# A selective scan in four engines: a product given to GpSimd, state copies given to ScalarE, and the order around the scans moved

## The chip, the cores and the metric

The kernel runs on one core of one Trainium2 chip. The metric is the device time of one execution, in microseconds (us). The core's engines run side by side, each in its own order of instructions: TensorE (PE: matmuls, PEld: weight loads), VectorE (DVE), ScalarE (ACT), GpSimd (POOL) and SyncE (SP), from whose queue the transfers are issued.

## The reference, cut to what matters

The program is four layers on an image of 2 x 64 x 256 x 256 numbers in float32, each added to its input. The change is in layer 1, which takes the 65536 pixels of each of the two images as a sequence and sends it through two Mamba blocks with a layer norm behind each:

```python
x = _mamba(x, p1_in_w, ...)
x = _layernorm(x, ln1_g, ln1_b)
x = _mamba(x, p2_in_w, ...)
x = _layernorm(x, ln2_g, ln2_b)
# inside _mamba: 128 channels d, 16 states n, step t
delta = jax.nn.softplus(xdbl[..., :dt_rank] @ dt_w.T + dt_b)
dA = jnp.exp(jnp.einsum('bld,dn->bldn', delta, A))
dBu = jnp.einsum('bld,bln,bld->bldn', delta, Bm, u)
def step(h, xs):
    dA_t, dBu_t, C_t = xs
    h = dA_t * h + dBu_t
    return (h, jnp.einsum('bdn,bn->bd', h, C_t))
y = jnp.moveaxis(ys, 0, 1) + u * D
y = y * _silu(res)
return y @ out_w.T
```

So every pair of channel and state has a recurrence over the sequence, h = dA * h + dBu, and each step's h is multiplied by C and summed over the states.

## The kernel before, in words

The sequence is cut into 128 chunks of T = 512 steps. A *task* is one block m (0 or 1) on one chunk; there are 256, in an order in which the two blocks alternate (the second runs three chunks behind), apart from a few at both ends. With few exceptions the odd tasks are those of the first block. A task has eight *groups* (b, j): b is the image, and j = 0 to 3 a quarter of the states. The 128 partitions hold 4 sets of states times 32 channels, and k = 0 to 3 goes over the remaining factor of the channels, so a group has four scans of 128x512.

A group's work:

- the product h = delta*u*B for all four k, 128x2048. For j = 0, 1, 3 it is DVE's (L773); B comes spread over the partitions by a matmul into `pb` (one buffer). For j = 2 it is POOL's (L755), made ahead by `product` behind the previous j = 3 (so three groups early), with B read from row 0 of the tile `cb`
- for each k: ACT makes `da` = exp(delta * A) (L789) into the pool `p_a`, which has three buffers; DVE scans (L792), from `da` and the product, in place in h
- POOL copies the last column of h as the state for this block's next chunk (`st`, L795), and multiplies h by C, in place (L796)
- one group later, at k = 3, `before()` has TensorE sum h over the states into `py` (four matmuls for the four k)

The tile h has five buffers. When all four groups of an image are in `py`, `gate` (L654, DVE) multiplies by Silu(res); it is called in the next image's group j = 1.

The rest of a block's work is laid between the groups by hand, by two generators: `front` prepares the task two ahead (convolution matmuls, Silu, Softplus, the spill of delta, delta*u, B and C to DRAM), and `layer_norm` ends the previous one. `aside(n)` has eight steps, one taken in each group by `next(steps)`, at k = 3 ahead of the exp. ACT's longer stretches there are called *bursts* here: Silu in group (0,3) (table load, `u` twice, `res` twice, table load for Exp), Softplus in (1,1) (table load, `delta` twice, the copy `bc`, table load), Square in (1,2), and Ln and Exp in (1,3) (two table loads). The norm's DVE product (L673) is in the next task's (0,0), behind the group's product, and the second block's statistics (L680) in its (0,1). POOL also has `du` = delta*u (L622) and the second block's residual add (L678).

The transfers back from DRAM (`fetch`) spread delta (`dl`), delta*u (`dv`) and five rows of B and C (`cb`) for the next task, on SP's queue, in (0,1) for b = 0 and in (1,1) for b = 1. Each engine's order in this loop is as it is written (`manual_schedule`).

Of the kernel before, what the change touches and what calls it, by code (L numbers as in the profile page):

```python
# [10 lines left out]
F32 = mybir.dt.float32  # L11
BF16 = mybir.dt.bfloat16
AF = mybir.ActivationFunctionType
ALU = mybir.AluOpType
# [3 lines left out]
P = 128  # L18
# [102 lines left out]
class Kernel:  # L121
# [405 lines left out]
    def layer1(self, x, y, coeffs):  # L527
        nc, tc, a = self.nc, self.tc, self.a
        T = SUB
        nch = HW // T  # L530
        stats = self.new_stats("stats_1")
        with ExitStack() as ctx:
            keep = ctx.enter_context(tc.tile_pool(name="l1k", bufs=1))
            ws = [self.mamba_weights(m, keep) for m in ("p1_", "p2_")]
# [9 lines left out]
            wide = ctx.enter_context(tc.tile_pool(name="l1w", bufs=3))  # L544
# [4 lines left out]
            p_a = ctx.enter_context(tc.tile_pool(name="l1pa", bufs=3, space=PSUM))  # L549
# [4 lines left out]
            for m in range(2):  # L554
                for b in range(2):
                    st = states.tile([P, 4, 4], F32, name=f"st{m}{b}", tag=f"st{m}{b}")
# [3 lines left out]
            def mm(out, lhsT, rhs, start=True, stop=True):  # L560
                nc.tensor.matmul(out, lhsT, rhs, start=start, stop=stop)  # L561
# [72 lines left out]
            def fetch(t, b):  # L634

                d_bc, d_dl, d_dv = t["spilt"]
                quads = [slice(32 * q, 32 * q + 32) for q in range(4)]
                for name, src in ("dl", d_dl), ("dv", d_dv):
                    s = t[name, b] = wide.tile([P, 4, T], F32, name=name)
                    for q in quads:  # L640
                        nc.sync.dma_start(s[q], src[b].rearrange("(d i) t -> d i t", i=4))

                c = t["cb", b] = wide.tile([P, 5, T], F32, name="cb")
                for i, q in enumerate(quads):
                    nc.sync.dma_start(
                        c[q].rearrange("p j t -> p (j t)"),
                        d_bc[b, 8 * i + 3 : 8 * i + 8]
                        .rearrange("j t -> (j t)")
                        .partition_broadcast(32),
                    )  # L650

            def gate(t, b):
                r = t["res"][b]
                nc.vector.tensor_tensor(r, r, t.pop("py"), ALU.mult)  # L654
# [30 lines left out]

            tasks = [(m, i - 3 * m) for i in range(nch + 3) for m in range(2)]
            tasks = [(m, i) for m, i in tasks if 0 <= i < nch]
            ts = [{} for _ in tasks]
            norm = iter(())

            def aside(n):

                nonlocal norm
                t = ts[n]
                ahead = front(*tasks[n + 2], ts[n + 2]) if n + 2 < len(tasks) else iter(())

                def d(b):
                    t["py"] = p_y.tile([P, T], F32, name="py")
                    mm(t["py"], ws[tasks[n][0]]["d"], t["u"][:, b], True, False)

                def more(b):
                    if n + 1 < len(tasks):
                        fetch(ts[n + 1], b)

                next(norm, None)
                next(ahead, None)
                yield
                d(0)
                next(norm, None)
                more(0)  # L710
                next(ahead, None)
                yield
                next(ahead, None)
                yield
                next(ahead, None)
                yield
                next(ahead, None)
                yield
                d(1)
                more(1)  # L720
                next(ahead, None)
                yield
                if n:
                    norm = layer_norm(*tasks[n - 1], ts[n - 1])
                next(norm, None)
                yield
                next(norm, None)
                yield
# [6 lines left out]
            with tc.manual_schedule(engines={E.PE, E.DVE, E.Activation, E.Pool, E.SP}):  # L735
                for b in range(2):
                    fetch(ts[0], b)


                groups = [(n, b, j) for n in range(len(tasks)) for b in range(2) for j in range(4)]  # L740
                direct = [(n, b, j) for n, b, j in groups if j != 2]
                rows = iter(direct)

                def spread():
                    n, b, j = next(rows, (None, None, None))
                    if n is None:
                        return None
                    pb = p_b.tile([P, T], F32, name="pb")
                    mm(pb, sel[:, b, j], ts[n]["bc"])
                    return pb  # L750

                def product(n, b, j):
                    t = ts[n]
                    h = pool.tile([P, 4, T], F32, name="h", bufs=5)
                    nc.gpsimd.tensor_tensor(  # L755
                        h,
                        t["dv", b],
                        t["cb", b][:, 0].unsqueeze(1).to_broadcast([P, 4, T]),
                        ALU.mult,
                    )  # L760
                    return h

                ahead = {2: product(*groups[2])}
                pb, before = spread(), None
                for g, (n, b, j) in enumerate(groups):
                    if b == j == 0:
                        steps = aside(n)
                    if j == 0:
                        st = states.tile([P, 4, 4], F32, name=f"st{tasks[n][0]}{b}")
                    t, m = ts[n], tasks[n][0]  # L770
                    if j != 2:
                        h = pool.tile([P, 4, T], F32, name="h", bufs=5)
                        nc.vector.tensor_tensor(  # L773
                            h, t["dv", b], pb.unsqueeze(1).to_broadcast([P, 4, T]), ALU.mult
                        )
                        pb = spread()
                    else:
                        h = ahead.pop(g)
                    if b == j == 0:
                        next(norm, None)  # L780
                    if j == 1 and g > 1:
                        gate(ts[n - 1 + b], 1 - b)
                    for k in range(4):
                        if k == 3:
                            next(steps)
                            if before:
                                before()
                        da = p_a.tile([P, T], F32, name="da")
                        nc.scalar.activation(  # L789
                            da, t["dl", b][:, k], AF.Exp, scale=ws[m]["a"][:, k, j : j + 1]  # L790
                        )
                        nc.vector.tensor_tensor_scan(  # L792
                            h[:, k], da, h[:, k], state[m, b][:, j, k : k + 1], ALU.mult, ALU.add
                        )
                    nc.gpsimd.tensor_copy(st[:, j], h[:, :, T - 1])  # L795
                    nc.gpsimd.tensor_tensor(  # L796
                        h, h, t["cb", b][:, 1 + j].unsqueeze(1).to_broadcast([P, 4, T]), ALU.mult
                    )
                    if g + 3 < len(groups) and j == 3:
                        ahead[g + 3] = product(*groups[g + 3])  # L800

                    def before(t=t, h=h, j=j):
                        for k in range(4):
                            mm(t["py"][32 * k : 32 * k + 32], quad, h[:, k], False, j == 3)

                    if j == 3:
                        state[m, b] = st
                before()
                gate(ts[-1], 1)
                for _ in norm:  # L810
                    pass
                for _ in layer_norm(*tasks[-1], ts[-1]):
                    pass
# [501 lines left out]
```

## Time and profile before

| | |
|---|---|
| median of three runs | 19872.43 us (19870.87 to 19875.25) |
| profiled execution: time, span | 19870.25 us, 19868.5 us |
| groups' loop of layer 1 in the trace | first product on DVE at 1738.76 us, last group's scans from 15904.47 us |
| DVE: products L773, scans L792 | 1536 and 8192, busy 3470.5 and 9837.4 us |
| POOL: C products L796, B products L755, copies L795 | 2048, 512 and 2048, busy 9255.6, 2319.8 and 387.3 us |
| ACT: exps L789 | 8192, busy 5564.8 us |
| TensorE's granted clock in layer 1 | 0.69 |

How to read a row of the profile: the line of the kernel, the engine, the operation, the tiles written and read, their shapes and the count; then busy time and the mean of one in ns; then the idle time of that engine just ahead of these instructions, with what released it. A row of the timeline begins with the start and the length in us; like instructions in a row are merged (x4), and the bracket holds the wait ahead of the first.

### The profile page before, as it was taken

The numbers are of one execution on the slowest core, as the hardware profiler recorded it, in microseconds if no ns is written. First come the engines' busy times: TensorE is split into PE (matmuls) and PEld (weight loads), VectorE is DVE, ScalarE is ACT, GpSimd is POOL, SyncE is SP. The second block draws the span as 40 slices with busy tenths as digits, with TensorE's granted clock in tenths as the row PEclk, the third lists the DMA queues.
The fourth block names the chain that finished last, engine by engine and source line by source line (L and its number), as shares of the span: only waits on it lengthen the run. The fifth ranks groups of instructions, "written<-read, shape, count | busy, mean of one in ns | idle before, by whom it ended". The sixth has DMA issues, their size and how long they took to land. (4 is left out here: it accounts for less than half of the span.)

```text
span 19868.5 us, 162340 instructions
## 1 busy us (share of the span) xinstructions
PE 14671.3 (74%) x48720; PEld 4849.2 (24%) x48720; DVE 18868.2 (95%) x16476; ACT 11805.5 (59%) x16810; POOL 15933.1 (80%) x7816
## 2 busy tenths in 40 slices
PE   6886777677767767677677767677777688888886
PEld 3332111111111111111111111111111144444444
DVE  7998999999999999999999999999999989999997
ACT  1224666666666666666666666666666655555554
POOL 4776888888888888888888888888888855555554
PEclk9997666666666666666666666666666689989998
DMA  3114666666666666666666666666666500000003
GB/s 118 47 46 110 152 152 153 151 154 150 155 148 157 147 157 147 157 148 156 149 154 151 153 152 153 152 153 151 152 151 152 136 29 29 29 29 29 29 27 144
DMA packets 662179, 2438.82 MB, mean 123 GB/s; under 512 B 131888, under 2 KB 201264, under 8 KB 450160
## 3 DMA queue, kind: packets, MB, share of 16 engines
q1 hardware_dynamic: 661296, 2428.43, 50.9%
q8 instruction: 385, 6.31, 0.1%
q14 instruction: 498, 4.08, 0.1%
HBM read 1990.14 MB, written 437.78 MB: 122 GB/s over the span
## 5 line engine op out<-in xcount | busy, mean ns | idle before, releaser
L792 DVE TENSOR_TENSOR_SCAN h<-da,st,h 128x512 f32<-128x512 f32 x8192 | 9837.4, 1262 | 309.0 <-ACT da L789 223.8
L796 POOL TENSOR_TENSOR h<-h,cb 128x2048 f32<-128x2048 f32 x2048 | 9255.6, 4519 | 166.0 <-POOL st L795 1.5
L789 ACT ACTIVATE da<-dl,p_a 128x512 f32<-128x512 f32 x8192 | 5564.8, 688 | 3985.3 <-DVE h L792 3892.6
L561 PE MATMUL py<-h,t_c_quad 128*32 128x512 f32 x16384 | 3254.7, 817 | 1656.9 <-POOL h L796 1655.9
L561 PE MATMUL pb<-bc,t_c_sel 64*128 64x512 f32 x3072 | 2696.9, 972 | 2379.9 <-DVE h L773 2374.3
L773 DVE TENSOR_TENSOR h<-dv,pb 128x2048 f32<-128x2048 f32 x1536 | 3470.5, 2259 | 40.2 <-DMA dv<-d_dv 40.2
L1021 POOL TENSOR_TENSOR gl<-gl,prod 128x512 f32<-128x512 f32 x1544 | 1961.1, 1271 | 1493.3 <-ACT prod L1017 1417.9
L755 POOL TENSOR_TENSOR h<-dv,cb 128x2048 f32<-128x2048 f32 x512 | 2319.8, 4531 | 16.3 <-DMA dl<-d_dl 16.3
L980 DVE SCALAR_TENSOR_TENSOR acc<-z,tap_b,acc 128x1024 f32<-128x1024 f32 (+1 forms) x1560 | 1987.3, 1274 | 38.8
L561 PEld LDWEIGHTS pb<-bc,t_c_sel 64*128 64x128 f32 x3072 | 661.0, 267 | 4406.4 <-DVE h L773 4339.5
L795 POOL COPY st<-h 128x4 f32<-128x4 f32 x2048 | 387.3, 189 | 1360.1 <-DVE h L792 1329.1
L561 PEld LDWEIGHTS py<-h,t_c_quad 128*32 128x32 f32 x16384 | 423.8, 122 | 3821.8 <-POOL h L796 3225.7
L561 PE MATMUL mm<-xin,p_conv 64*128 64x512 f32 x4096 | 1321.1, 774 | 15.4 <-DMA x1t<-y 15.4
L1064 PE MATMUL pcv<-z,diag 128*128 128x512 f32 x2322 | 1172.0, 622 | 20.4 <-ACT gl L1072 16.6
L1017 ACT ACTIVATE prod<-z,tap_a 128x512 f32<-128x512 f32 x1544 | 1045.0, 714 | 37.6 <-POOL gl L1021 37.4
L949 ACT COPY z<-pz 128x512 f32<-128x512 f32 x768 | 456.8, 599 | 1027.3 <-PE pz L941 924.8
L941 PE MATMUL pz<-t_c_inv,gf 128*128 128x128 f32 (+1 forms) x8192 | 1038.5, 309 | 1.4 <-ACT z L949 1.0
L941 PEld LDWEIGHTS pz<-t_c_inv,gf 128*128 128x128 f32 (+1 forms) x8192 | 848.3, 181 | 517.4 <-issue 311.9
L561 PE MATMUL mm<-u,p_dt 128*128 128x512 f32 x1024 | 931.3, 1064 | 0.0
L561 PE MATMUL py<-u,p_d 128*128 128x512 f32 x1024 | 820.9, 895 | 0.0
L915 PE MATMUL f<-t_w_inT,xf 64*128 64x384 f32 x2048 | 597.0, 615 | 156.4 <-DVE gf L922 155.5
L561 PEld LDWEIGHTS mm<-xin,p_conv 64*128 64x128 f32 x4096 | 459.7, 244 | 982.5 <-issue 982.3
(166 smaller groups left out, 17767.8 us busy)
## 6 DMA issues: line engine op xcount, KB each, us to landing
cb<-d_bc SPq DMA_DIRECT2D x2048, 320.0 KB
dl<-d_dl SPq DMA_DIRECT2D x2048, 256.0 KB
dv<-d_dv SPq DMA_DIRECT2D x2048, 256.0 KB
d_dl<-delta SPq DMA_DIRECT2D x256, 512.0 KB
d_dv<-du SPq DMA_DIRECT2D x256, 512.0 KB
xin<-in_x SPq DMA_DIRECT2D x16, 2048.0 KB
xt<-in_x SPq DMA_DIRECT2D x32, 1024.0 KB
y<-yt SPq DMA_DIRECT2D x128, 256.0 KB
```

Of the source, the lines that this page charges most:

```text
L561: nc.tensor.matmul(out, lhsT, rhs, start=start, stop=stop)
L755: nc.gpsimd.tensor_tensor(h, t["dv", b], t["cb", b][:, 0].unsqueeze(1).to_broadcast([P, 4, T]), ALU.mult,)
L773: nc.vector.tensor_tensor(h, t["dv", b], pb.unsqueeze(1).to_broadcast([P, 4, T]), ALU.mult)
L789: nc.scalar.activation(da, t["dl", b][:, k], AF.Exp, scale=ws[m]["a"][:, k, j : j + 1])
L792: nc.vector.tensor_tensor_scan(h[:, k], da, h[:, k], state[m, b][:, j, k : k + 1], ALU.mult, ALU.add)
L796: nc.gpsimd.tensor_tensor(h, h, t["cb", b][:, 1 + j].unsqueeze(1).to_broadcast([P, 4, T]), ALU.mult)
L915: nc.tensor.matmul(p, x_f[t][half, g], w_in[half], start=True, stop=True)
L941: nc.tensor.matmul(pz[i * n : (i + 1) * n, k, :, 16 * g : 16 * g + 16], gf[t, 2 * e + g, b][:, c0 : c0 + n], inv, start=True, stop=True,)
L980: eng.scalar_tensor_tensor(out, near(s, name, m0, r, k), w, box["t"], ALU.mult, ALU.add)
L1017: nc.scalar.activation(prod, near(s, name, 4 * h + m, n, k), AF.Copy, scale=w)
L1021: nc.gpsimd.tensor_add(acc, acc, prod)
L1064: nc.tensor.matmul(box["t"], diag[:, k], near(s, f"a{i}", 4 * h + m, n, k), start=k == 0, stop=k == 8,)
```

## The change

1. In every second task (n odd) POOL also makes the product of the group (1,0), ahead, behind its work for group (0,1). B's first row for it comes by four transfers of its own into a tile `b0` (`t["first"]`), in `fetch` for b = 1.
2. The copy of the last states goes from POOL to ACT. With POOL's product with C (and with a product made ahead) it is put in a function `tail`, which runs in the next group at k = 2, ahead of that exp.
3. `gate` goes from ahead of the scans of group j = 1 to between its second and third scan.
4. In each group the fourth exp is issued ahead of `next(steps)` and `before()`, no longer behind them.

```diff
+                if b and t["n"] % 2:
+                    own = t["first"] = wide.tile([P, T], F32, name="b0", bufs=1)
+                    for i, q in enumerate(quads):
+                        nc.sync.dma_start(own[q], d_bc[b, 8 * i].partition_broadcast(32))
...
-            ts = [{} for _ in tasks]
+            ts = [{"n": n} for n in range(len(tasks))]
...
+                def pooled(n, b, j):
+                    return j == 2 or (n % 2 == 1 and b == 1 and j == 0)
...
-                direct = [(n, b, j) for n, b, j in groups if j != 2]
+                direct = [group for group in groups if not pooled(*group)]
...
-                        t["cb", b][:, 0].unsqueeze(1).to_broadcast([P, 4, T]),
+                        (t["cb", b][:, 0] if j == 2 else t["first"])
+                        .unsqueeze(1)
+                        .to_broadcast([P, 4, T]),
...
-                    if j != 2:
+                    if not pooled(n, b, j):
...
-                    if j == 1 and g > 1:
-                        gate(ts[n - 1 + b], 1 - b)
                     for k in range(4):
+                        if k == 2:
+                            if j == 1 and g > 1:
+                                gate(ts[n - 1 + b], 1 - b)
+                            if tail:
+                                tail()
+                        da = p_a.tile([P, T], F32, name="da")
+                        nc.scalar.activation(
+                            da, t["dl", b][:, k], AF.Exp, scale=ws[m]["a"][:, k, j : j + 1]
+                        )
                         if k == 3:
                             next(steps)
                             if before:
                                 before()
-                        da = p_a.tile([P, T], F32, name="da")
-                        nc.scalar.activation(
-                            da, t["dl", b][:, k], AF.Exp, scale=ws[m]["a"][:, k, j : j + 1]
-                        )
                         nc.vector.tensor_tensor_scan(
                             h[:, k], da, h[:, k], state[m, b][:, j, k : k + 1], ALU.mult, ALU.add
                         )
-                    nc.gpsimd.tensor_copy(st[:, j], h[:, :, T - 1])
-                    nc.gpsimd.tensor_tensor(
-                        h, h, t["cb", b][:, 1 + j].unsqueeze(1).to_broadcast([P, 4, T]), ALU.mult
-                    )
-                    if g + 3 < len(groups) and j == 3:
-                        ahead[g + 3] = product(*groups[g + 3])
+
+                    def tail(g=g, t=t, h=h, b=b, j=j, st=st):
+                        nc.scalar.copy(st[:, j], h[:, :, T - 1])
+                        nc.gpsimd.tensor_tensor(
+                            h,
+                            h,
+                            t["cb", b][:, 1 + j].unsqueeze(1).to_broadcast([P, 4, T]),
+                            ALU.mult,
+                        )
+                        if g + 3 < len(groups) and pooled(*groups[g + 3]):
+                            ahead[g + 3] = product(*groups[g + 3])
...
+                tail()
                 before()
```

More of the change, by code (lines that the diff above doesn't have):

```diff
@@ L763, in layer1 @@
                 ahead = {2: product(*groups[2])}
-                pb, before = spread(), None
+                pb, before, tail = spread(), None, None
                 for g, (n, b, j) in enumerate(groups):
```

## The prediction

> **What bounds the kernel now.** I read the page first: which engine is full, and for how long in layer 1.
>
> ```profile
> PE 14671.3 (74%) x48720; PEld 4849.2 (24%) x48720; DVE 18868.2 (95%) x16476; ACT 11805.5 (59%) x16810; POOL 15933.1 (80%) x7816
> DVE  7998999999999999999999999999999989999997
> L792 DVE TENSOR_TENSOR_SCAN h<-da,st,h 128x512 f32<-128x512 f32 x8192 | 9837.4, 1262 | 309.0 <-ACT da L789 223.8
> L773 DVE TENSOR_TENSOR h<-dv,pb 128x2048 f32<-128x2048 f32 x1536 | 3470.5, 2259 | 40.2 <-DMA dv<-d_dv 40.2
> L755 POOL TENSOR_TENSOR h<-dv,cb 128x2048 f32<-128x2048 f32 x512 | 2319.8, 4531 | 16.3 <-DMA dl<-d_dl 16.3
> ```
>
> VectorE (DVE) is full; in layer 1 only the 224 us behind exps (`da`) and, in the list of DVE's waits from 2500 to 15900 us, 186 us of gates behind `py` are idle. So the time is DVE's work plus its stalls. Next the timeline of one odd task around its group (0,3), where the Silu burst of ScalarE (ACT) lies, and (1,1), where the Softplus burst lies; (b,j) names a group.
>
> ```profile
> 9008.86 2.26 DVE L773 TENSOR_TENSOR h<-dv,pb 128x2048 f32<-128x2048 f32 x1
> 9008.97 0.69 ACT L789 ACTIVATE da<-dl,p_a 128x512 f32<-128x512 f32 x1 [0.48 <-DVE h L792]
> 9009.68 1.28 ACT L601 ACT_TABLE_LOAD   x1
> ...
> 9011.22 3.63 DVE L792 TENSOR_TENSOR_SCAN h<-da,st,h 128x512 f32<-128x512 f32 x3
> ...
> 9014.79 2.73 ACT L789 ACTIVATE da<-dl,p_a 128x512 f32<-128x512 f32 x4
> ...
> 9015.51 1.28 DVE L792 TENSOR_TENSOR_SCAN h<-da,st,h 128x512 f32<-128x512 f32 x1 [0.66 <-ACT da L789]
> ...
> 9019.08 4.81 DVE L792 TENSOR_TENSOR_SCAN h<-da,st,h 128x512 f32<-128x512 f32 x4
> 9020.39 0.69 ACT L789 ACTIVATE da<-dl,p_a 128x512 f32<-128x512 f32 x1 [2.87 <-DVE h L792]
> ...
> 9023.80 2.26 DVE L773 TENSOR_TENSOR h<-dv,pb 128x2048 f32<-128x2048 f32 x1
> 9024.63 1.28 ACT L525 ACT_TABLE_LOAD   x1
> ...
> 9026.73 0.69 DVE L654 TENSOR_TENSOR res<-res,py 128x512 f32<-128x512 f32 x1 [0.67 <-PE py L561]
> 9027.33 9.50 DVE L792 TENSOR_TENSOR_SCAN h<-da,st,h 128x512 f32<-128x512 f32 x8
> 9028.96 0.69 ACT L789 ACTIVATE da<-dl,p_a 128x512 f32<-128x512 f32 x1
> ```
>
> All constants come from these rows, start to start. Product to scan 2.36 (9008.86 to 9011.22); a scan 1.18 (four from 9019.08 to the product at 9023.80); first scan's start to the exp it frees 1.31 (9020.39: `p_a` has three buffers, so a group's fourth exp waits for its first scan); exp 0.69; Silu burst from table load to next exp 5.11 (9009.68 to 9014.79); Softplus burst 4.33 (9024.63 to 9028.96); exp start to scan 0.72 (9014.79 to 9015.51). A gate costs 0.42 behind a product (9051.33 product, 9054.11 scan, against 2.36), but a 128x512 DVE instruction between two scans, the statistics at 9057.66, costs 0.58 to the scan at 9058.24; with rounding I take 0.59. From an odd task's product of (0,3) at 4025.40 to that at 9008.86, 90 tasks later, the mean task is 55.37 us.
>
> **What the skill says of these rows.** "ScalarE: Activation LUTs", section "What ACT_TABLE_LOAD costs", charges every change of table set a load of about 1283 ns and a drain, 2.66 us in all. The trace has the load (1.28) but the next activation starts 1.30 after it (9010.98), with no drain ahead of it; I use the trace's burst lengths. "GPSIMD Engine Reference", section 3.1, gives 4497 ns on GpSimd (POOL) and 2293 ns on DVE for a two-input 2048-element operation; the trace agrees (4531 and 2259), so moving a product saves DVE 2.36 with its gap and costs POOL 4.5.
>
> **The change, part by part.** In each, t = 0 is DVE's start on the product of (0,3).
>
> *Third product on POOL, and the Silu burst.* DVE loses one product in odd tasks: 128 x 2.36 = 302 us of work. The place matters: it is (1,0), the group behind the Silu burst. Before, the burst followed the third exp, at 0.82, and the stall was one of 0.66 at the fourth scan; the first scan of (1,0) started at 10.22. Now the fourth exp goes first: first scan 2.36, +1.31 = 3.67, exp to 4.36, burst at 4.38, next exp 4.38 + 5.11 = 9.49, scan of (1,0) at 10.21. DVE has finished its scans at 2.36 + 4.72 = 7.08. In an even task the product of (1,0) fills to 9.44: stall 0.77. In an odd task nothing stands there: stall 3.13. In both the scan starts at 10.21, as before. So the 2.36 saved becomes wait: gain 0.
>
> *Softplus burst.* Before, product and gate of (1,1), then three scans, covered it with no stall. From the first scan of (1,0) to the first of (1,2): 4.72 + 2.36 + 0.42 + 4.72 = 12.22, plus the gate's wait for `py` (0.67, 0.38, 0.16, 1.40 in four tasks from 9000, mean 0.65) = 12.87. Now: scans of (1,0) from 10.21 free DVE at 14.93; product, first scan of (1,1) at 17.29; fourth exp at 18.60 to 19.29; burst 19.31 + 4.33 = 23.64; exp, scan of (1,2) at 24.36. DVE itself is done at 17.29 + 4.72 + gate 0.59 = 22.60, and (1,2) has no product, being POOL's already: stall 1.76. The stretch is 14.15: +1.28 per task.
>
> *Rest of the task.* (1,2), (1,3), (0,0), (0,1), (0,2) hold 20 scans, three products, one norm product (0.42), the gate now at 0.59: 23.60 + 7.08 + 0.42 + 0.59 = 31.69, and 0.59 of statistics in every second task. The Ln burst is still covered: fourth exp of (1,3) ends at 33.44 (its first scan 24.36 + 4.72 + 2.36 = 31.44), burst 3.83 (9037.58 to 9041.41), exp done 37.98, while the scan of (0,0) comes at 38.94 behind a product. Gained here: 0.57, in two of those four tasks, of a fourth scan of (1,2) behind the Square; lost 0.17 of gate: -0.11.
>
> *Sum.* Odd 10.21 + 14.15 + 31.69 + 0.59 (the statistics fall in its stretch) = 56.64; even 56.05; mean 56.35, against 55.37: +0.98. (The parts add to 1.16: the mean of 90 tasks holds 0.18 of small waits that four tasks don't show, and I go by it.) Some 254 tasks hold both bursts: +249 us. The profiled execution took 19870.25 us (span 19868.5 and 1.75 around it), 2 under the median of the three runs: 20119 from it, 20121 from the median. I say 20120.
>
> *State copies on ACT.* 2048 small copies leave POOL (189 ns each, about 0.26 with the gap) and join ACT. Nearest ACT rows: 202 ns for 128x1, 216 for 128x16; the skill's 186 ns + 0.833 per element bounds it below, the 64x512 copy's 569 ns above. I take 0.21. It stands ahead of the next group's third exp, which waits for the same scan anyway, and DVE has a spare 0.78 there even behind the Silu stall: 0 on the path. But POOL's product with C overwrites what the copy reads, so it now waits for ACT: for (0,3) the copy ends at 11.09, not just after the last scan at 7.2; for (1,3) at 38.9 instead of 36.3.
>
> *POOL with its cover.* From 11.15, with 4.47 a product and 2.30 for `du` (9030.82 to 9033.12): C of (0,3), B of (1,2) done at 20.1, needed at 22.6 to 24.4; C of (1,0), `du`, C of (1,1) done 31.4; TensorE's `py` and the next `pb` done 35.4, product of (0,0) at 36.16: cover 0.75. C of (1,3) 38.95, B of (0,2) done 48.0, needed 51.3; the residual add 49.3, statistics at 50.15: cover 0.85. The extra product in an odd task ends at 5.9 of 10.2. Without these covers each us late costs DVE a us per task, 254 us. The gate at 19.65 finds `py` done at about 17.6.
>
> *DMAs.* Four on SP's queue for B's first row, 64 KB each, in every second task, about 0.43 us to issue each (four took 1.69 at 9021.68). Behind them waits the spill of `bc`, which waits for ACT longer; landing has over 30 us. Cost 0; +33.5 MB on 2438.82.
>
> **Rivals.**
> (a) The bursts are hidden, as four exps ahead would suggest. Then all 7.42 us of stalls per pair of tasks (3.13 + 0.77 + 2 x 1.76) go: 112.69 - 7.42 = 105.27 against 110.74, 128 x -5.47 = -700: 19170. Half of it, only the product's 302, gives 19570. It decides if the fourth exp doesn't wait for the first scan of its group, or a burst is under 3 us. Against: the exp at 9020.39 waits 2.87 for that scan, and the bursts measure 5.11 and 4.33.
> (b) POOL is late: copies held up by bursts, one more product, and about 100 us of work (21 products at 4.47, two `du`, an add of 1.26) in a pair of 112.7. Above 0.75 us late, the product of (0,0) waits; 1 us beyond costs 254: about 20370.
> (c) The change does little: a Softplus stall shorter by 1 us leaves 19870. For it speaks only the cost of a gate between scans, which is 0.6 of cover and counted already. That the order isn't what it says: the built order has the product with B's own row on POOL in odd tasks alone, 640 in all, so no.
>
> **How the numbers follow.** Mine 0.82 (20120), (a) 0.07, (b) 0.08, (c) 0.03. The stalls are differences of durations that vary by 0.02, but there are four joints per task; 0.4 us per task either way is 100 us, and (b) reaches in from above: 20020 to 20260. A measurement here tells about 0.2%, 40 us, from no change: faster 0.07, same 0.03, slower 0.90.
>
> **What the profile after should show.** Scans of (1,0) starting behind a gap of about 3.1 us in odd and 0.8 in even tasks, those of (1,2) behind 1.8 in all, all put down to `da`; DVE's wait for `da` near 3.7 x 255 = 940 us; no gap at the fourth scan of (0,3); gate waits near none; DVE products 1408, 289 us less busy; POOL waiting for ACT's copies. I am wrong if the gap in odd tasks is as in even ones, if (1,2) starts without one, or if products wait for `pb`.

## The result, and the profile after

The changed kernel takes 20219.03 us (median of four runs, 20211.53 to 20221.18) against 19873.76 us (also the median of four): the ratio is 1.0173, 95% interval 1.0158 to 1.0188. The forecast was 20120 in 20020 to 20260. The profiled execution has a span of 20217.2 us.

The page after, its engines and the groups that answer to those shown before (busy us and mean ns, then idle time just ahead and what ended it):

```profile
PE 14814.0 (73%) x48464; PEld 4812.0 (24%) x48464; DVE 18601.0 (92%) x16348; ACT 11886.4 (59%) x18858; POOL 16116.0 (80%) x5896
...
L805 DVE TENSOR_TENSOR_SCAN h<-da,st,h 128x512 f32<-128x512 f32 x8192 | 9879.9, 1264 | 1120.5 <-ACT da L798 568.5
L811 POOL TENSOR_TENSOR h<-h,cb 128x2048 f32<-128x2048 f32 x2048 | 9222.6, 4517 | 1685.6 <-ACT st L810 1539.7
...
L783 DVE TENSOR_TENSOR h<-dv,pb 128x2048 f32<-128x2048 f32 x1408 | 3183.0, 2261 | 41.2 <-DMA dv<-d_dv 41.2
...
L810 ACT COPY st<-h 128x4 f32<-128x4 f32 x2048 | 387.1, 189 | 559.2 <-DVE h L805 559.2
```

DVE works 267 us less and the kernel takes 345 us longer: its idle time ahead of scans grew from 309 to 1120 us. DVE's timeline shows where, with some rows of ScalarE. First come the Silu and Softplus stretches of an even task (the product of its group (0,3) is at 9018.66), then those of the odd task behind it (from 9074.82):

```profile
9018.66 2.26 DVE L783 TENSOR_TENSOR h<-dv,pb 128x2048 f32<-128x2048 f32 x1
...
9028.88 4.81 DVE L805 TENSOR_TENSOR_SCAN h<-da,st,h 128x512 f32<-128x512 f32 x4 [0.87 <-ACT da L798]
...
9037.29 0.69 ACT L798 ACTIVATE da<-dl,p_a 128x512 f32<-128x512 f32 x1 [2.78 <-DVE h L805]
9038.00 1.28 ACT L525 ACT_TABLE_LOAD   x1
...
9043.13 4.81 DVE L805 TENSOR_TENSOR_SCAN h<-da,st,h 128x512 f32<-128x512 f32 x4 [1.75 <-POOL h L811]
...
9074.82 2.26 DVE L783 TENSOR_TENSOR h<-dv,pb 128x2048 f32<-128x2048 f32 x1
9077.19 4.81 DVE L805 TENSOR_TENSOR_SCAN h<-da,st,h 128x512 f32<-128x512 f32 x4
...
9082.83 0.60 ACT L606 ACTIVATE res<-mm 128x512 f32<-128x512 f32 x1 [0.56 <-PE mm L561]
...
9085.53 4.81 DVE L805 TENSOR_TENSOR_SCAN h<-da,st,h 128x512 f32<-128x512 f32 x4 [3.53 <-ACT da L798]
...
9099.77 4.81 DVE L805 TENSOR_TENSOR_SCAN h<-da,st,h 128x512 f32<-128x512 f32 x4 [1.74 <-POOL h L811]
```

The exp at 9037.29 is a fourth one: it has waited 2.78 us for its group's first scan, and only then does the Softplus burst begin. That is so throughout: in all 1875 groups of this trace from 2500 to 15800 us the fourth exp starts 1.29 to 1.32 us behind the start of its group's first scan. In the odd task the scans at 9077.19 are those of the group (0,3), nothing stands between them and (1,0), and DVE waits 3.53 us.

### The profile page after: what moved, and what is told of

Same layout as the page of the kernel before. It is cut to its first block, busy times and chain, and to the rows that moved or that the text cites. A ratio compares the mean times of both kernels' runs of the same rounds, so it can differ in the third digit from the quotient of the medians.

```text
span 20217.2 us, 161828 instructions
## 1 busy us (share of the span) xinstructions
PE 14814.0 (73%) x48464; PEld 4812.0 (24%) x48464; DVE 18601.0 (92%) x16348; ACT 11886.4 (59%) x18858; POOL 16116.0 (80%) x5896
## 5 line engine op out<-in xcount | busy, mean ns | idle before, releaser
L783 DVE TENSOR_TENSOR h<-dv,pb 128x2048 f32<-128x2048 f32 x1408 | 3183.0, 2261 | 41.2 <-DMA dv<-d_dv 41.2
L561 PE MATMUL pb<-bc,t_c_sel 64*128 64x512 f32 x2816 | 2252.6, 891 | 637.9 <-DVE h L783 636.2
L561 PE MATMUL py<-u,p_d 128*128 128x512 f32 x1024 | 918.6, 994 | 750.3 <-DVE res L658 750.3
L561 PEld LDWEIGHTS pb<-bc,t_c_sel 64*128 64x128 f32 x2816 | 565.2, 250 | 2471.6 <-DVE h L783 2077.3
L561 PE MATMUL mm<-xin,p_res 64*128 64x512 f32 x1024 | 608.1, 677 | 628.5 <-ACT u L601 628.5
L561 PE MATMUL mm<-u,p_dt 128*128 128x512 f32 x1024 | 837.4, 965 | 0.0
L810 ACT COPY st<-h 128x4 f32<-128x4 f32 x2048 | 387.1, 189 | 559.2 <-DVE h L805 559.2
```

The costliest lines, as they stand in the source:

```text
L783: nc.vector.tensor_tensor(h, t["dv", b], pb.unsqueeze(1).to_broadcast([P, 4, T]), ALU.mult)
```

## The experiments

Ratios are to the kernel before, timed beside each run, with their 95% intervals. Six kernels answer one table. All of them have the copies on ScalarE and the gate two scans down. The columns are without and with the third product; the rows are the place of the bursts.

| bursts | without the third product | with it |
|---|---|---|
| ahead of the fourth exp (old) | 19767.95 us, 0.9948 (0.9933 to 0.9963) | 19944.41 us, 1.0039 (1.0024 to 1.0054) |
| behind the fourth exp (new) | 20205.07 us, 1.0169 (1.0153 to 1.0184) | 20219.03 us, 1.0173 (the change) |
| mixed: ahead in (0,3) and (1,1) alone | 19743.10 us, 0.9939 (0.9923 to 0.9956) | 19622.46 us, 0.9875 (0.9860 to 0.9890) |

**The order alone, on the kernel before.**

```diff
-                        if k == 3:
-                            next(steps)
-                            ...
                         da = p_a.tile([P, T], F32, name="da")
                         nc.scalar.activation(...)
+                        if k == 3:
+                            next(steps)
+                            ...
```

> The kernel before with part 4 of the change alone: the fourth exp ahead of next(steps) and before(). Theory: the Silu stretch stays 10.2 to 10.5 us; in (1,1) the gate ahead of the scans delays the fourth exp by 0.4 us, the Softplus stretch takes 14.6 plus the gate's wait of about 0.65 against 12.9 before; the 0.57 behind the Square goes: about +2.1 us a task, 20340 to 20480 us. Rival (the order costs nothing, the loss is in the copies, the gate or POOL): 19870.

Measured: 20436.40 us, ratio 1.0286 (1.0269 to 1.0304). The gap ahead of (1,2), 2.35 by the prediction's constants with the gate ahead of the scans, is 2.34 us in 192 of the 231 tasks from 2500 to 15800 us of the trace. The order by itself costs 569 us, more than the whole change. Two of the expected parts missed in opposite ways: the mean Silu stretch is 10.96 us in even and 10.81 in odd tasks, not 10.2 to 10.5, and the Softplus stretch 14.89 and 14.95, not 14.6 plus 0.65. Why the first is longer is said below, under the mis-sized term.

**The changed kernel with the old order.** The same edit the other way round.

> The changed kernel with part 4 alone undone: next(steps) and before() stand ahead of the fourth exp again. Theory (the fourth exp waits for its group's first scan, so the burst starts 3.6 us later and loses the product that covered it): in odd tasks the Silu stall falls from 3.3 to about 0.7 us and lies at the fourth scan of (0,3), the Softplus stall of 1.75 goes. By hand: to the first scan of (1,0) 7.88 us in odd and 10.22 in even tasks, then 12.39, then about 31.97, and 0.3 of statistics: 53.7 us a task against 56.7, so about 19450 us for the whole. Rival (POOL is late, through copies on ScalarE and the third product): the stalls behind the POOL product stay, about 20200. Rival (the loss is the copies and the gate): about 20200 as well.

Measured: 19944.41 us. Undoing the order takes back 275 of the 345 us, and the gaps ahead of (1,2) are gone; but I had expected 19450. The timelines of GpSimd, TensorE, ScalarE and DVE in an odd task of this run show where the 500 us are:

```profile
9063.09 4.50 POOL L811 TENSOR_TENSOR h<-h,cb 128x2048 f32<-128x2048 f32 x1
...
9067.64 1.94 PE L561 MATMUL py<-h,t_c_quad 128*32 128x512 f32 x8 [3.23 <-POOL h L811]
...
9069.51 1.97 PE L561 MATMUL mm<-res,p_out 128*64 128x512 f32 x4
...
9071.58 0.60 ACT L666 ACTIVATE lsq<-mm 128x512 f32<-128x512 f32 x1 [5.16 <-PE mm L561]
...
9072.80 1.28 DVE L805 TENSOR_TENSOR_SCAN h<-da,st,h 128x512 f32<-128x512 f32 x1 [3.67 <-ACT da L802]
```

POOL, with one more product in its queue, ends its product with C of (1,0) at 9067.6; only then can TensorE make `py`, and behind it in TensorE's queue stand the two matmuls that Square reads. Square stands ahead of the fourth exp of (1,2) again, so the scan waits 3.67 us. That wait has a mean of 3.54 us in the odd tasks from 2500 to 15800 us, and 0.06 in the run without the third product (19767.95 us). So the third product is lost here too, to another wait; the table says that it even costs 176 us.

**The change without the third product.**

```diff
-                if b and t["n"] % 2:
+                if False:
...
-                    return j == 2 or (n % 2 == 1 and b == 1 and j == 0)
+                    return j == 2
```

> The changed kernel without the third product: VectorE makes the product of (1,0) in odd tasks too (and b0 isn't fetched). Theory (in this order the product of (1,0) only filled the Silu stall, so giving it away gained nothing): odd tasks become like even ones, 20190 to 20260 us. Rival (the product saved its 302 us, and other parts lost 650): 20520. Rival (the third product makes POOL late and costs): below 20150.

Measured: 20205.07 us (20196.56 to 20218.44), inside the theory's range and not to be told from 20219. So the 302 us of work that DVE gave away bring nothing in this order.

**The change with the copies back on GpSimd.**

```diff
-                        nc.scalar.copy(st[:, j], h[:, :, T - 1])
+                        nc.gpsimd.tensor_copy(st[:, j], h[:, :, T - 1])
```

> The changed kernel with the state copies back on GpSimd (in tail, at the same place). Theory: POOL's product with C no longer waits for ScalarE behind a burst, but VectorE waits for exps, not for POOL: 20219, within 40 us, with the gaps of 1.75 ahead of (1,2) unchanged. Rival (those gaps are POOL's lateness, as the releaser in the trace names it): they shrink by some of the 3.6 us by which POOL starts earlier on (0,3), and the time falls by up to 430 us.

Measured: 20218.85 us, ratio 1.0176 (1.0159 to 1.0193). The waits of DVE from 2500 to 16200 us, of this run (us in total, times, longest):

```profile
DVE h L805 <- ACT da L798: 749.0, 362, 4.1
DVE h L805 <- POOL st L810: 210.0, 120, 1.8
```

The same list of the changed kernel:

```profile
DVE h L805 <- ACT da L798: 537.9, 241, 4.1
DVE h L805 <- POOL h L811: 422.1, 241, 2.1
```

The sums are 959.0 and 960.0. In the changed kernel POOL's product with C ends within 0.1 us of the scan of (1,2) in nearly every task; with the copies on POOL it ends 1.1 us or more ahead of it, and the gap stays at 1.75. So the name of POOL in the bracket at 9043.13 marks what had ended last, not the cause.

**Copies and gate alone** (the changed kernel with the old order and without the third product).

> The changed kernel with parts 1 and 4 undone: what is left beside the kernel before is the copies on ScalarE (with POOL's work in tail) and the gate two scans down. Theory: the gates' waits for py (0.77 us a task) go, a gate between scans costs 0.17 more each (0.34), the 0.57 behind Square may go: like the even tasks of the run with the old order, 54.75 us a task, 19700 to 19760 us. Rival (copies on ScalarE delay POOL and with it py and Square): 19870 or more.

Measured: 19767.95 us: 103 us faster than the kernel before, and 8 us above the range. The gates' waits for `py` are gone from DVE's list; the stall at the fourth scan of (0,3) stays (0.81 in most tasks). No run has the copies or the gate alone, so how the 103 us fall to the two is not shown. An estimate puts them on the gate: its waits were 204.7 us in the trace before and are 6.9 here, and by the prediction's 0.17 a gate its new place costs about 0.34 x 254 = 86 us.

**The gate back up.**

```diff
-                        if k == 2:
-                            if j == 1 and g > 1:
-                                gate(ts[n - 1 + b], 1 - b)
-                            if tail:
-                                tail()
+                        if k == 0 and j == 1 and g > 1:
+                            gate(ts[n - 1 + b], 1 - b)
+                        if k == 2 and tail:
+                            tail()
```

> The changed kernel with the gate back ahead of the scans of group j = 1. Theory: in (1,1) the gate then stands ahead of the scan that frees the fourth exp's buffer, so the Softplus stall is 2.34 as in the kernel before with the new order, not 1.75; it costs 0.17 less at two places: +0.25 us a task and the gate's waits for py, 20280 to 20390. Rival (the gate's place is only a matter of its wait for py, which is gone): 20130 to 20220.

Measured: 20388.30 us, ratio 1.0262 (1.0247 to 1.0277). The Softplus gap is 2.34 or 2.35 us in 228 of the 232 tasks from 2500 to 15800 us of the trace. Most of the rest of the loss, beyond the 0.25 x 254 = 64 us of that step, is in Silu gaps, which reach 4.07: the burst's last Silu waits longer for TensorE. In this run from 2500 to 15500 us, and then in the changed kernel from 2500 to 16200:

```profile
ACT res L606 <- PE mm L561: 175.1, 198, 1.1
ACT res L606 <- PE mm L561: 73.4, 115, 1.1
```

**A buffer of its own for the fourth `da`**, on the changed kernel and on the one before.

```diff
-                    raw[i] = io.tile([P, T], F32, name="x1t", bufs=3)
+                    raw[i] = io.tile([P, T], F32, name="x1t", bufs=2)
...
-                        da = p_a.tile([P, T], F32, name="da")
+                        da = (
+                            pool.tile([P, T], F32, name="da3", bufs=1)
+                            if k == 3
+                            else p_a.tile([P, T], F32, name="da")
+                        )
```

> The changed kernel with the order kept, but each fourth da in a buffer of its own (one more, in SBUF; one buffer less for x1t makes room). So the fourth exp waits no longer for the first scan of its group, only for the last scan of the group before. Theory: both bursts then start about 1 us after the group's start, and all stalls behind da go: 52.6 us a task, 19170 us, if POOL keeps up (about 100 us of work in a pair of 105); 19170 to 19400. Rival (POOL is what (1,2) waits for, as the releaser in the trace names it): the 1.75 us ahead of (1,2) stay, 19600 to 19700. Rival (POOL's total decides): gaps move to the products and gates, over 19700.

> The kernel before with the same buffers as in the run with a buffer of its own for the fourth da: a control for what the buffer in SBUF costs or brings by itself. Theory: the burst stands ahead of that exp here, so its buffer sets nothing: 19874, within 40 us. If reading da from SBUF slows the scan or the exp by 0.05 us, 2048 of them make 100 us more.

Measured: 22156.50 us (1.1153, 1.1136 to 1.1169) and 21881.09 us (1.1013, 1.0997 to 1.1030). Both expectations missed. In the changed kernel DVE's list of waits from 3000 to 16000 us is empty, as the theory said, but neither a time nor the cause can be read from it: scans that read `da` from SBUF take longer here, and longer scans also give every burst more cover. (That the buffer is the wait rests on the 1875 groups above and on the runs with the order alone.) The control shows the slower scans. Its row for the tile `da` (min/median/max ns of the scans, a quarter of which read from SBUF):

```profile
L796 DVE TENSOR_TENSOR_SCAN h<-da,st,h x6583: 1246/1259/4604, 3000.0 to 15999.2; 128x512 f32<-128x512 f32 x200
```

And its timeline around a group of four, with GpSimd beside it:

```profile
9040.93 4.52 POOL L800 TENSOR_TENSOR h<-h,cb 128x2048 f32<-128x2048 f32 x1
...
9042.88 8.13 DVE L796 TENSOR_TENSOR_SCAN h<-da,st,h 128x512 f32<-128x512 f32 x4
...
9045.42 4.51 POOL L755 TENSOR_TENSOR h<-dv,cb 128x2048 f32<-128x2048 f32 x1
```

Four scans took 8.13 us where 4.81 is usual, and end at 9051.01, 1.08 us behind POOL's second product (9045.42 + 4.51 = 9049.93). Of the 1645 fourth scans from 3000 to 16000 us, 618 took under 1.3 us, as scans with `da` in PSUM do; each of the other 1027 ends 1.07 to 1.09 us behind the end of a POOL instruction. That agrees with "SBUF — State Buffer" in the Trainium skill, section "SBUF: two separate sides", by which a DVE instruction with two SBUF inputs and a GpSimd instruction that reads SBUF lock each other out for a whole instruction. The longest scan, 4604 ns, is 1259 and 3.3 us of a 4.5 us product. The other half of the edit, a buffer less for `x1t`, shows in no wait of DVE's in this stretch.

**The mixed order.** Each burst is put where its cover is: Silu and Softplus, whose next group may have no product on DVE, ahead of the fourth exp; Square, Ln and the rest behind it.

```diff
+                        early = (b, j) in ((0, 3), (1, 1))
+                        if k == 3 and early:
+                            next(steps)
+                            ...
                         da = p_a.tile([P, T], F32, name="da")
                         nc.scalar.activation(...)
-                        if k == 3:
+                        if k == 3 and not early:
                             next(steps)
```

> The changed kernel with the old order (bursts ahead of the fourth exp) in groups (0,3) and (1,1) alone, that is for Silu and Softplus, whose next group may have no product on VectorE; Square, Ln and the rest stay behind the fourth exp. Theory after the run with the old order everywhere, where the 3.5 us at the fourth scan of (1,2) in odd tasks came from Square waiting for matmuls behind GpSimd: Square now has the product of (1,3) as its cover, the Silu stall is about 0.8 to 1.2 at the fourth scan of (0,3), Softplus and Ln have none. Odd tasks about 53.1, even about 54.5 us: 53.8 a task, 19430 to 19600 us, below both kernels. Rival (POOL, with its 100 us of work a pair, sets the pace as soon as the bursts don't): gaps behind POOL's product or py, 19700 to 19950.

> The kernel with the mixed order (bursts ahead of the fourth exp in (0,3) and (1,1) alone) without the third product. Theory: in this order the third product gives back 2.36 us in each odd task less what its lateness costs there (1.1 behind Square, some 0.5 behind pb): about 0.9 x 128 = 110 us lost without it, 19690 to 19760. Rival (the third product brings nothing in any order): 19620. Rival (it brings all its work): 19920.

Measured: 19622.46 us with the third product, 19743.10 without. With it, this is faster than the kernel before by 1.25% and than the changed one by some 600 us. It misses its range by 22 us. What is left in its list of DVE's waits from 2500 to 15500 us:

```profile
DVE h L810 <- ACT da L803: 322.5, 314, 1.8
DVE h L783 <- PE pb L561: 65.0, 84, 1.0
```

The second line is the cover of 0.75 us ahead of the product of (0,0), which the prediction named: in this faster kernel it fails, always in the task behind an odd one, and without the third product no product waits for `pb`. The third product is worth 121 us here, of the 302 of its work.

**The matmuls that Square reads, one group earlier** in the mixed order.

```diff
                     mm(po[C * b : C * b + C], ws[m]["out"], t["res"][b])
+                yield
...
                 next(ahead, None)
-                yield
                 if n:
                     norm = layer_norm(*tasks[n - 1], ts[n - 1])
+                next(norm, None)
+                yield
                 next(norm, None)
                 yield
```

> The kernel with the mixed order and the third product, with the two matmuls that Square reads (po) issued one group earlier, in (1,1), ahead of the matmuls of (1,0) into py that wait for GpSimd. Theory: Square no longer waits behind POOL's product with C, the gaps of about 1.1 us behind it in odd tasks go: 128 x 1.1 = 140 us less than 19622, 19450 to 19560. Rival (po then waits for Softplus's buffer and makes py, pb and the products late): 19620 or more.

Measured: 19679.24 us, ratio 0.9907 (0.9892 to 0.9921): slower than the mixed order by 57 us. Square's waits for TensorE are gone from ScalarE's list (549.7 us in the mixed order, 2500 to 15500 us), and the rival came true, since the waits for `pb` grew from 65.0 to 168.4 us:

```profile
DVE h L812 <- ACT da L805: 265.1, 238, 1.3
DVE h L785 <- PE pb L561: 168.4, 120, 1.4
```

**TensorE kept busy ahead of the Silu burst** (see the mis-sized term below).

```diff
-                    mm(pb, sel[:, b, j], ts[n]["bc"])
+                    for _ in range(times):
+                        mm(pb, sel[:, b, j], ts[n]["bc"])
...
-                        pb = spread()
+                        pb = spread(3 if (b, j) == (0, 3) else 1)
```

> The changed kernel with the matmul into pb that stands ahead of the Silu burst (group (0,3)) issued three times over, with the same result: TensorE is idle for less time ahead of the second half's res matmul, on which the last Silu of the burst waits. In the changed kernel's trace that pair of matmuls takes 1.12 us where TensorE sat idle up to 2.5 us ahead of it, and 1.12 to 2.07 (mean 1.50) where it sat idle 2.5 to 3.2 us. Theory (the longer idle time slows the matmul, and that is what makes the Silu burst longer than the 5.11 taken from before): every pair takes 1.12, the Silu gaps are 0.87 in even and 3.12 in odd tasks, and 0.27 us a task go: 255 x 0.27 = 70 us less than 20219, about 20150. Rival (the matmul is late for another reason, such as its buffer or the queue): 20219, or more for the added work.

Measured: 20207.03 us (20202.54 to 20219.30), ratio 1.0171 (1.0157 to 1.0185): not to be told from 20219. The idle time ahead of the matmul fell below 1.5 us, and it is slow all the same: 1.12 to 2.07 us, mean 1.61, in the 43 cases of the trace from 5000 to 12000 us with 1 to 1.5 us of idle time. The theory, that the length of the idle time by itself makes the matmul slow, fell.

## Why the prediction was right

Step by step, against the trace after:

- *Silu stretch*, from the product of (0,3) to the first scan of (1,0), 10.21 in both: 10.22 in the even task shown, 10.71 in the odd one, and 10.29 in the next odd one (9188.22 to 9198.51). The product saved became a wait, as the run without the third product shows.
- *Softplus stretch*, 14.15: 9028.88 to 9043.13 is 14.25. The scan on POOL's product starts 0.80 us behind its exp (9042.33), where I took 0.72; it is 0.79 or 0.80 in 349 of the 353 groups from 2500 to 15800 us whose product POOL made and whose first scan starts behind a gap ((1,2), and (1,0) in odd tasks), and 0.72 at (1,0) in even tasks.
- *Rest of the task*, 31.69: 9043.13 to 9074.82 is 31.69; with statistics 9099.77 to 9132.06, 32.29 against 32.28.
- *Task*: 56.73 us over 244 tasks (gates at 2061.0 and 15902.6) against 56.35 forecast; before it was 55.37. From 2500 to 15800 us the mean change of a task is +0.26 us in the Silu stretch, +1.16 in the Softplus stretch and -0.07 in the rest, where the prediction had 0, +1.28 and -0.11.
- *Copies, gate, DMAs*: a copy takes 189 ns (0.21 forecast) and moves nothing (20218.85 us with the copies back on POOL). The lower bound in the prediction is an estimate from the Trainium skill, "ScalarE: Activation LUTs", section "What ACT_TABLE_LOAD costs", whose formula for an ACTIVATE gives 186 + 4 x 0.833 = 189 ns; the trace agrees. The gates' waits fell from 204.7 us to 8.2, and the transfers grew by 33.55 MB.

**The mis-sized term.** The sum said +249 us, the chip +345; a task takes 0.38 us more than forecast. Of it 0.10 is the Softplus stretch and 0.04 the Silu stretch of odd tasks, through scans that start 0.79 or 0.80 us behind their exp, not 0.72. The rest, 0.23, is the Silu burst. I took it as 5.11 us because it was so before (5.10 to 5.13 from 2500 to 15800 us); in the changed kernel it is 5.10 to 6.06, mean 5.34. It holds a joint with TensorE that the prediction left out: the last Silu waits for the second half's `res` matmuls, which need the buffer that the first `u` frees. Before, they were in time (1.4 us of waiting in all); now ScalarE waits 78.1 us for them.

What makes that pair of matmuls slow is in the trace's record of the granted clock. Three pairs of the changed kernel: the stretch and its length, TensorE's busy time, and then PEclk, the share of full speed granted (the last two columns are of DMAs).

```profile
core 0: us, PE busy (x), PEclk, DMA share, GB/s
9420.89:9422.01 1.12, 1.12 (x2) 1.00 1.10 234
9081.25:9082.79 1.54, 1.54 (x2) 0.69 1.01 218
9477.72:9479.77 2.05, 2.04 (x2) 0.51 0.98 210
```

From 5000 to 12000 us this trace has 123 such pairs. The 46 that took over 1.2 us had a mean granted clock of 0.87 or less, the other 77 of 0.89 or more. In the kernel before TensorE comes to the pair without a pause, and all 126 ran at 1.00 in 1.12 us; so did all 129 in the mixed order. With the order alone 108 of 121 pairs were slow, with the gate back up 106 of 122, always at the lower clock: these are the longer Silu stretches of those two runs. So the new order leaves TensorE idle ahead of the pair (1.4 to 3.0 us; up to 3.3 with the order alone), and the granted clock, which is 1.0 or 0.5 at any moment of this record, can fall to half before the pair is done. The Trainium skill's "TensorE: Matmul & The Clock Gate", Part 1, halves the clock after an idle window of about 3.4 us. These gaps don't reach that, and the clock fell all the same. In this record it changes at whole multiples of 3.41 us, and in the 3.41 us ahead of its 351 falls TensorE was busy for 13 to 60% (mean 38%); where it stayed at 1.0, for 45 to 100% (mean 85%). The extra matmuls of the last run raised the first mean to 49% and left 334 falls. Where the border lies stays open, and no run moved the clock by itself.

The forecast was right in its mechanism: the order makes the fourth exp wait, and the product saved turns into that wait. That its number falls inside the range is in part luck, since the missing 0.38 us uses up nearly all of the 0.4 us a task that the range allowed, and 0.23 of it comes from a joint with TensorE that the prediction did not have.

The expected label on the gaps was wrong in half of the cases (all those ahead of (1,2): POOL's product instead of `da`), and rival (b) was not seen: the products found `pb` in time. But the cover of 0.75 us was real, since it fails in the mixed order, where the tasks are shorter. Rival (a), with all bursts hidden, would have needed the third product to be worth its work of 302 us, and no order tried gives it more than 121: with it Square waits for POOL's later results in the old order, and the product of (0,0) waits for `pb` in the mixed one.

## What to carry to other kernels

A look-ahead is counted in buffers, not in instructions issued: with three buffers, a fourth exp placed ahead of a long stretch makes it wait for the first consumer, and trades the work that stood ahead for the work that stands behind. Before an instruction is taken off the full engine, ask what waits it was covering; before a long stretch on another engine is moved, list what the full engine has to do from its new start to its end. A releaser's name in a trace is a guess to be tried by moving that work: here it was POOL's in half the gaps, and they stayed when POOL's work moved. And a burst's length measured in one order holds for another only if everything that it waits for stays in time: here a pair of matmuls did not.

## What the runs showed that I had not expected

A scan whose two tensors are both in SBUF took up to 4604 ns beside GpSimd's products, against a median of 1259 over all scans, and a quarter of the scans changed in this way made the kernel before 2014 us slower (19867.42 to 21881.09). And the same pair of small matmuls took from 1.12 us at full clock to 2.07 at half, in a stretch where TensorE had paused for 3 us at most.
